# Graph convolution with a highway gate on one core: sort rooms, one visit for the orders, later adding transfers, one flag for two branches

## Chip, cores and metric

The kernel runs on one core of one Trainium2 chip, in one launch. The metric is the device time in microseconds (us) of one execution; for the kernel before, three runs were taken and the median counts. A profiled execution is a further one, with its own time.

## The reference

`x` has N = 1250 rows of D = 1024 floats. There are 20000 edges `src -> dst`, sorted by `dst`, each with one of R = 8 types. Cut to what matters:

```python
h = jnp.maximum(_layernorm(x, axis=-1), 0.0)
u = h @ root + bias
for r in range(R):                        # 8 relations
    mask = (edge_type == r)
    sums = segment_sum(h[src] * mask[:, None], dst, num_segments=N)
    cnt  = segment_sum(mask, dst, num_segments=N)
    u = u + (sums / jnp.maximum(cnt, 1.0)[:, None]) @ weight[r]
z = concatenate([u, h], axis=1) @ w_gate + b_gate
return x + jnp.tanh(u) * z + h * (1.0 - z)
```

## The kernel before

**The products.** Each relation's product `y = h @ weight[r]` is made for all rows first; the edges then gather rows of `y` and add them up with a weight each. There are eleven matrices, numbered `s`: 0 to 7 the relations, 8 `root`, 9 the lower half of `w_gate` (`LAST`), 10 its upper half, which needs `u`. Matrix 0 and matrix 10 go block by block through `product` (five blocks of 256 rows, seven half-size products each, `A11` to `S4`, with the sums `t1` to `t4` of the matrix's quarters as factors). Matrices 1 to 9 go through `kind(m, n, between)`, seven kinds each, written (s, n) here: one kind is one of the seven products of Strassen's scheme for all blocks, and most kinds use the scheme a second time inside. A kind takes about 15.5 us of TensorE time. Its line 330 (`add`) issues the matmuls; line 438 (`tensor_add(banks[2 * u][:, H:], ...)`) adds an inner product onto an accumulator bank on VectorE, which later matmuls of the same kind continue; lines 276 to 283 make the inner sums, line 238 the next factor, lines 346 to 388 move finished banks to rows; line 288 stores and line 296 loads the "lefts", sums of the left operand kept in `lefts_dram`. `store_rows` (line 484) puts finished rows on SyncE's queue.

**What runs beside.** The order of instructions is written out by hand: every `kind` calls `call(k)` for k = 0 to 4, and generators that hang there issue a few instructions at each visit. `at_call` holds the place. In order of time these generators are: the layer norms and the index (`norms_and_index`), the counts of each node's edges per relation (`beside_group`, `counts(g)`), the branch for nodes with more edges than the 22 slots of the table (`counts_over`), the weights of the edges (`weights_of_groups`), and the edges themselves in three groups of relations (`edges(g, ...)`, groups 0, 1, 2), with a gather on GpSimd (line 1407, five buffers `got`) and an add on VectorE (line 1412) for each slot.

**The index.** `order()` sorts the nodes by their number of edges, for each group. Its tiles come from a pool `sort`, opened after the pool `ix0` is closed; so they lie over `raw`, `bits` and `pool_of` of that pool. The table of edges is written from `bits` by one DMA on GpSimd's queue (line 1215). `nodes_in_order` then makes, for one group, an equality matrix on VectorE, waits until `at_call[2] == 2`, turns it with ten matmuls into a bank `ps_q` (line 804), and issues ten gathers of table rows into `idx` (line 728, in `rows_of`). After each group, three or four transfers `out += h` with `accum_op` follow on GpSimd's queue (line 1237, ten in all).

**The flags.** `any_over` reduces, by a transpose on TensorE and a maximum, the largest edge count into `n_far`; `counts_over` loads it into every engine's registers and branches (line 1702) before kind (3,0). Ahead of it, what is left of the counts is issued in one go (lines 1386 and 769 to 774):

```python
            if (s, i) == (BEGIN[0], BEGIN[1] - 1):
                for _ in ready:
                    pass
                counts_over()
```

A second flag `n_pass` is made in `passes_needed` from the weights behind each row's K slots (30 reductions, line 1498) and branches before kind (8,5) (line 1753).

**The gate.** In matrix 9, `beside_kind` loads the quarters of matrix 10 and makes `t1` (line 202), `t2` (line 206), `t3` (line 210) at calls 1, 2, 3 of kind 6; `make_t4` is line 214. In `product`, `p2`, `p3`, `p7` add `A12`, `S4` and `S3`; copies on ScalarE free the bank `ps_b` (lines 612, 628, 636, 639). `gate_h` gathers rows of `h`, `gate_d` makes tanh(u) on ScalarE (line 1857), which writes into a tile that rows of `z` leave by DMA; `gate_turned` transposes `u`, with copies at lines 538 and 540.

Of the kernel before, what the change touches and what calls it, by code (L numbers as in the profile page):

```python
# [21 lines left out]
def tile_rgcn_highway(  # L22
# [139 lines left out]
    class Factors:  # L162
# [12 lines left out]
        def load_first(self, k=slice(0, KQ)):  # L175
# [129 lines left out]
    def kind(m, n, between):  # L305
# [56 lines left out]
        def to_rows_of(odd):  # L362
            of = [(i, banks[i]) for i in (odd, odd + 2)]
            for i, b in of:
# [33 lines left out]
        if chained:  # L398
# [101 lines left out]
    def beside_kind(m, n, k):  # L500
# [15 lines left out]
        elif (n, k) == (5, 0):  # L516
            gate.load_b22()
        elif (n, k) == (6, 0):
            gate.load_b21()
        elif (n, k) == (6, 1):  # L520
            gate.make_t1()
        elif (n, k) == (6, 2):
            gate.make_t2()
        elif (n, k) == (6, 3):
            gate.make_t3()
# [48 lines left out]
    def product(aop, w, to, between=lambda j: None, last=None, pieces=1, second=None, third=None,  # L574
# [76 lines left out]
        else:  # L651
            d = p7()
# [66 lines left out]
    n_pass = const.tile([1, 1], I32, name="n_pass")  # L719
# [59 lines left out]
    def nodes_in_order(g, pos, ids_f, a, b, small, many):  # L779

        a = a[:, :KEYS].rearrange("p (c q) -> p c q", q=P)
        b = b[:, :2 * ND * ND].rearrange("p (c d) -> p c d", d=2 * ND)
        hi_i, lo, hi, block = [small[:, P + k * ND:P + (k + 1) * ND] for k in range(4)]
        hi_i, lo, hi = hi_i.bitcast(I32), lo.bitcast(I16)[:, :ND], hi.bitcast(I16)[:, :ND]
        nc.vector.tensor_copy(block, many[:, :ND])
        nc.vector.tensor_copy(hi_i, pos)  # L788
        nc.vector.tensor_single_scalar(hi_i, hi_i, 7, op=OP.arith_shift_right)
        nc.vector.tensor_copy(hi, hi_i)  # L790
        nc.vector.scalar_tensor_tensor(lo, hi_i, float(-P), pos, op0=OP.mult, op1=OP.add)
        nc.vector.tensor_tensor(a, lo[:, :, None].to_broadcast([P, ND, P]),
                                many[:, None, :].to_broadcast([P, ND, P]), op=OP.is_equal)
        nc.vector.tensor_tensor(b[:, :, :ND], hi[:, :, None].to_broadcast([P, ND, ND]),
                                many[:, None, :ND].to_broadcast([P, ND, ND]), op=OP.is_equal)
        nc.vector.tensor_tensor(b[:, :, ND:], b[:, :, :ND],
                                block[:, :, None].to_broadcast([P, ND, ND]), op=OP.mult)
        nc.vector.tensor_scalar(b[:, :, :ND], b[:, :, :ND], ids_f[:, :1], None, op0=OP.mult)
        yield
        while at_call[2] != 2:  # L800
            yield
        p = sum_bank("ps_q")
        for c in range(ND):
            nc.tensor.matmul(p[:, :2 * ND], a[:, c], b[:, c], start=(c == 0), stop=(c == ND - 1))
        nc.vector.tensor_copy(lo_f := small[:, P + 4 * ND:P + 5 * ND], p[:, :ND])
        nc.vector.scalar_tensor_tensor(node[:, g, :], p[:, ND:2 * ND], float(P), lo_f,
                                       op0=OP.mult, op1=OP.add)
        nc.vector.tensor_single_scalar(node_key[:, g, :], node[:, g, :], g * KEYS, op=OP.add)
        for d in range(ND):
            rows_of(idx[:, g, d, :], table_rows, node_key[:, g, d:d + 1])  # L810
# [113 lines left out]
    def largest(*pairs):  # L924
        p = sum_bank("ps_q")
# [1066 lines left out]
```

## Time and profile before

| | |
|---|---|
| time, median of 3 runs | 1289.37 us (1286.6 to 1289.46) |
| profiled execution, its own time | 1283.34 us |
| span from first to last instruction | 1281.5 us |
| mean granted TensorE clock | 0.996 of full speed |
| TensorE (PE) matmul busy | 1249.9 us, 98% |
| VectorE (DVE) busy | 970.8 us, 76% |
| GpSimd (POOL) busy | 443.7 us, 35% |
| ScalarE (ACT) busy | 274.4 us, 21% |

The profile names engines PE (matmul), PEld (weight load), DVE, ACT, POOL and SP; L438 is line 438 of the kernel before. A row of a timeline gives the start, the busy time, the engine, line and operation, what it writes and reads, how many, and in brackets the idle time just before and what ended it. A row of windows gives the stretch, its length, the busy time of the engines with their instructions, the granted clock (1.00 is full), the mean busy share of the 16 DMA engines and the GB/s moved. A row of waits gives the engine, the waiting instruction's tile and line, what it waited for, and the total in us, the number of times and the longest. The span is 1.8 us shorter than the execution's own time.

### The profile page before, as it was taken

How to read it: one execution, taken by the hardware profiler on the slowest of the kernel's cores; microseconds unless marked ns; L12 is line 12 of the kernel's file. 1: busy time of each engine (PE TensorE's matmuls, PEld its weight loads, DVE VectorE, ACT ScalarE, POOL GpSimd, SP SyncE). 2: the span in 40 equal slices, each digit the busy share in tenths (PEclk: the TensorE clock that was granted, in tenths of full speed). 3: DMA queues.
4: the chain of work that ended last, by engine and by line, in shares of the span. 5: the costliest groups of instructions: out<-in, count | busy, mean ns of one | idle time of the engine just before them, and what ended most of it. 6: DMA issues, size and time to landing. Idle time of an engine off the chain costs nothing.

```text
span 1281.5 us, 14045 instructions
## 1 busy us (share of the span) xinstructions
PE 1249.9 (98%) x4725; PEld 883.1 (69%) x4725; DVE 970.8 (76%) x1462; ACT 274.4 (21%) x517; POOL 443.7 (35%) x400
## 2 busy tenths in 40 slices
PE   9999999899989999999999999999999999999996
PEld 5444777677767777777777777777777777544443
DVE  7545898786579787887878779898888799766642
ACT  3452211121122112112111211211221121202210
POOL 1330000028202222322431333453442558854531
PEclk9999999999999999999999999999999999999999
DMA  7965445838946686898898768899995949999973
GB/s 303 195 191 163 156 149 195 242 107 211 294 149 224 205 280 222 321 335 305 287 341 281 251 197 294 294 331 352 365 301 204 349 141 342 346 333 228 234 150 57
DMA packets 130432, 317.87 MB, mean 248 GB/s; under 512 B 30999, under 2 KB 32222, under 8 KB 130190
## 3 DMA queue, kind: packets, MB, share of 16 engines
q1 hardware_dynamic: 85726, 186.64, 42.7%
q0 software_dynamic: 44336, 129.72, 34.3%
q8 instruction: 38, 0.62, 0.2%
q10 hardware_dynamic: 288, 0.52, 0.1%
q14 instruction: 44, 0.36, 0.1%
HBM read 258.79 MB, written 90.18 MB: 272 GB/s over the span
## 4 chain that ended last, share of the span: by engine, by line
PE 43%; issue 10%; DMA 7%; POOL 7%; DVE 2%; POOLq 0%; ACT 0%; DVEq 0%; SPq 0%; ACTq 0%
PE ps_n L330 14%; PE ps L330 14%; PE ps_b L337 9%; DMA got<-y,idx 5%; PE ps_q L330 4%; POOL got L1407 3%; DMA z_dram<-w 2%; PE ps_b L589 1%; POOL h_all L728 1%; POOL out_dram L739 1%; POOL u L728 1%; PE ps_n L589 1%; POOL w L728 0%; DVE h_all L1412 0%; DVE u L1412 0%
## 5 line engine op out<-in xcount | busy, mean ns | idle before, releaser
L1407 POOL DMA_INDIRECT got<-y,idx x205 | 256.0, 1249 | 435.5 <-DVE u L1412 332.6
L330 PE MATMUL ps<-w,h_all 128*128 128x256 f32 (+1 forms) x1040 | 258.7, 392 | 0.0
L1412 DVE SCALAR_TENSOR_TENSOR u<-got,w_of,u 128x1024 f32<-128x1024 f32 (+1 forms) x189 | 241.5, 1280 | 12.4 <-DMA got<-y,idx 9.8
L330 PE MATMUL ps_n<-w,w 128*128 128x256 f32 x976 | 234.2, 383 | 9.2 <-DVE ps L438 7.3
L330 PEld LDWEIGHTS ps_n<-w,w 128*128 128x128 f32 x976 | 185.0, 191 | 63.2 <-issue 22.2
L337 PE MATMUL ps_b<-w,h_all 128*128 128x512 f32 x504 | 226.6, 592 | 0.0
L330 PEld LDWEIGHTS ps<-w,h_all 128*128 128x128 f32 x1040 | 197.4, 190 | 39.6 <-issue 14.1
L337 PEld LDWEIGHTS ps_b<-w,h_all 128*128 128x128 f32 x504 | 95.8, 190 | 94.1 <-issue 90.9
L589 PE MATMUL ps_b<-w,h_all 128*128 128x512 f32 x312 | 139.4, 593 | 4.4 <-DVE w L206 2.6
L330 PE MATMUL ps_q<-w,w 128*128 128x256 f32 x488 | 116.8, 383 | 5.4 <-DMA w<-lefts_dram 5.4
L448 ACT COPY ps<-ps_n 128x512 f32<-128x512 f32 x122 | 64.8, 575 | 252.5 <-PE ps_n L330 209.1
L330 PE MATMUL ps<-w,w 128*128 128x256 f32 x488 | 115.6, 380 | 0.0
L330 PE MATMUL ps_n<-w,h_all 128*128 128x256 f32 x488 | 115.3, 379 | 0.0
L589 PEld LDWEIGHTS ps_b<-w,h_all 128*128 128x128 f32 x312 | 58.6, 190 | 77.4 <-issue 73.0
L438 DVE TENSOR_TENSOR ps<-ps_n,inner 128x256 f32<-128x256 f32 x122 | 50.5, 430 | 75.0 <-PE ps L330 67.8
L330 PEld LDWEIGHTS ps_q<-w,w 128*128 128x128 f32 x488 | 93.1, 191 | 19.4 <-DVE w L388 4.8
L330 PEld LDWEIGHTS ps<-w,w 128*128 128x128 f32 x488 | 93.1, 191 | 12.8
L330 PEld LDWEIGHTS ps_n<-w,h_all 128*128 128x128 f32 x488 | 92.7, 190 | 13.0 <-issue 0.5
L424 ACT COPY ps<-ps_n 128x256 f32<-128x256 f32 x122 | 39.7, 361 | 247.0 <-PE ps_n L330 178.6
L238 DVE TENSOR_TENSOR w<-w,w 128x2048 f32<-128x2048 f32 x36 | 82.3, 2287 | 0.3
L589 PE MATMUL ps<-w,h_all 128*128 128x512 f32 (+1 forms) x136 | 57.6, 567 | 0.0
L728 POOL DMA_INDIRECT idx<-table,node_key x30 | 32.5, 1082 | 58.6 <-DVE small L788 47.9
(247 smaller groups left out, 1154.8 us busy)
## 6 DMA issues: line engine op xcount, KB each, us to landing
w<-lefts_dram SPq DMA_DIRECT2D x102, 512.0 KB
w<-in_L_gnn_weight_dram SPq DMA_DIRECT2D x31, 1024.0 KB
y<-row SPq DMA_DIRECT2D x84, 256.0 KB
y<-w SPq DMA_DIRECT2D x42, 256.0 KB
w<-in_L_gnn_w_gate_dram SPq DMA_DIRECT2D x8, 1024.0 KB
lefts_dram<-w SPq DMA_DIRECT2D x14, 512.0 KB
h_dram<-h_all SPq DMA_DIRECT2D x9, 512.0 KB
y<-row SPq DMA_DIRECT2D x9, 512.0 KB
```

The source lines that it names most:

```text
L238: nc.vector.tensor_sub(w[to], w[a], w[b])
L330: nc.tensor.matmul(p, a[:, k], b[:, k], start=(fresh and k == 0), stop=(k == a.shape[1] - 1), skip_group_check=True)
L337: nc.tensor.matmul(to, h_op[NP - 1][:, ORDER[n], k], w[:, k], start=(fresh and k == 0), stop=(k == KQ - 1), skip_group_check=True)
L424: nc.scalar.copy(banks[2 * u][:, :H], xs[u])
L438: nc.vector.tensor_add(banks[2 * u][:, H:], xs[u], ys[:, u * H:(u + 1) * H])
L448: nc.scalar.copy(banks[2 * u + 1].rearrange("p (a n) -> p a n", a=2), xs[u][:, None, :].to_broadcast([P, 2, H]))
L589: nc.tensor.matmul(b[:, at], aop[:, i, k, :], w.of[i][:, k, at], start=(fresh and k == 0), stop=(k == KQ - 1), skip_group_check=True)
L728: nc.gpsimd.indirect_dma_start(out=to, out_offset=None, in_=of, in_offset=bass.IndirectOffsetOnAxis(ap=at, axis=0), compute_op=op)
L739: ins = nc.gpsimd.indirect_dma_start(out=of, out_offset=bass.IndirectOffsetOnAxis(ap=at, axis=0), in_=frm, in_offset=None, compute_op=op)
L1407: nc.gpsimd.indirect_dma_start(out=t[:n], out_offset=None, in_=y[g][:, :], in_offset=bass.IndirectOffsetOnAxis(ap=at[:n, d, k:k + 1], axis=0),
L1412: nc.vector.scalar_tensor_tensor(u[:n], t[:n], w, u[:n], op0=OP.mult, op1=OP.add)
```

## The change

The edit has seven parts.

1. The sort's tiles are views of `raw` and of `pool_of` (the latter now allocated next to `bits`), not of a pool of their own; `ix0` is closed after the order.
2. `nodes_in_order` prepares the matrices of all three groups, and turns all of them in one visit, with thirty matmuls into one bank; then the thirty gathers follow, ten a visit.
3. The ten `out += h` transfers are issued by `with_ready`, at each third slot of the edges from slot 12 on, beginning in group 0.
4. `beyond` compares, before the weights are made, the index behind each row's K slots with a constant (fifteen small operations) and takes its maximum into the same `most` column as the edge count; `any_over` sends that column through DRAM to one row (two DMAs on GpSimd's queue), so that `n_far` stands for both branches. The counts are issued one group a visit; `counts_over` is placed before kind (3,1) in place of (3,0); the weights come beside the first slots of group 0.
5. `t1` and `t2` of matrix 10 lie in other buffers, and `t1`, `t2`, `t3` are made at call 3 of kind 5 and calls 1 and 2 of kind 6. A kind without inner scheme empties its second bank one call earlier.
6. `gate_h` and `gate_d` of a block come at j = 5, behind `gate_turned`; block 0's `gate_d` moves into the gate's product.
7. In the last block `p2` comes just before `p7`, not in second place.

```diff
@@ Factors.load_first
-                self.place = dict(b11=old["a"], t3=old["e"], b22=old["b"], t1=old["d"],
-                                  t2=rights, b21=lefts, t4=old["c"])
+                self.place = dict(b11=old["a"], t3=old["e"], b22=old["b"], t1=rights,
+                                  t2=old["d"], b21=lefts, t4=old["c"])
@@ kind, chained part
                 if i == 2:
                     to_rows_of(0)
+                if i == 3:
+                    to_rows_of(1, (0,))
...
-            to_rows_of(1)
+            to_rows_of(1, (2,))
@@ beside_kind
-        elif (n, k) == (6, 1):
+        elif (n, k) == (5, 3):
             gate.make_t1()
-        elif (n, k) == (6, 2):
+        elif (n, k) == (6, 1):
             gate.make_t2()
-        elif (n, k) == (6, 3):
+        elif (n, k) == (6, 2):
             gate.make_t3()
@@ product, last block
         else:
+            p2()
             d = p7()
             last(d, 0)
             p3()
@@ nodes_in_order: all groups prepared, then
+        p = sum_bank("ps_q")[:, :2 * G * ND].rearrange("p (g d) -> p g d", g=G)
+        for g, (a, b, lo_f) in enumerate(parts):
+            for c in range(ND):
+                nc.tensor.matmul(p[:, g], a[:, c], b[:, c], start=(c == 0), stop=(c == ND - 1))
...
+        for g in range(G):
+            for d in range(ND):
+                rows_of(idx[:, g, d, :], table_rows, node_key[:, g, d:d + 1])
+            yield
@@ any_over
-        largest((most[:, 2:3], bad))
+        row = const.tile([1, P], F32, name="bad_row")
+        nc.gpsimd.dma_start(val_dram[0, :P, None], most[:, 2:3])
+        nc.gpsimd.dma_start(row, val_dram[:1, :P])
+        for _ in range(3):
+            yield
+        nc.vector.reduce_max(bad, row, axis=AX.X)
@@ order
-            with tc.tile_pool(name="sort", bufs=1) as sp:
-                counted.extend([sp.tile([P, NHI * NCNT // n], F32, name=f"counted{k}")
...
-                    for d in range(g * ND // G, (g + 1) * ND // G):
-                        nc.gpsimd.dma_start(out[block(d)], h_dram[block(d)], accum_op=OP.add,
-                                            max_dma_last_dim=4 * D)
+            a, b = raw.bitcast(F32), pool_of.bitcast(F32)
+            m = NHI * NCNT
+            counted.extend([a[:, :m], a[:, m:m + m // 2], a[:, m + m // 2:2 * m]])
@@ beside_group
-            yield
             for g in range(G):
-                yield from counts(g)
+                for _ in range(3):
+                    yield
+                for _ in counts(g):
+                    pass
+            yield
+            yield from beyond()
+            yield from any_over()
@@ beyond (new)
+                    nc.vector.tensor_single_scalar(
+                        flags[:, used:used + n].rearrange("p (g d) -> p g d", d=e - d),
+                        idx[:, gs[0]:gs[-1] + 1, d:e, k], float(FAR), op=OP.is_lt)
...
+            nc.vector.reduce_max(most[:, 1:2], flags, axis=AX.X)
+            nc.vector.tensor_max(most[:, 2:3], most[:, 2:3], most[:, 1:2])
@@ the loop over kinds
-            if (s, i) == (BEGIN[0], BEGIN[1] - 1):
-                for _ in ready:
-                    pass
-                counts_over()
-                ready = weights_of_groups()
+        assert next(ready, 0) == 0
+        far = load(n_far)
+        counts_over(far)
+        ready = weights_of_groups()
@@ with_ready
-            for _ in e:
+            for t, _ in enumerate(e):
                 next(ready, None)
+                if added and t > late + GOT and t % 3 == 0:
+                    nc.gpsimd.dma_start(*added.pop(), accum_op=OP.add, max_dma_last_dim=4 * D)
                 yield
@@ second branch
-        passes = nc.values_load(n_pass[0:1, 0:1], ...)
-        with tc.If(passes > 0):
+        with tc.If(far > 0):
@@ gate
-            if i == 0 and j == 4:
-                gate_z(0)
+            if i == 0 and j in (2, 4):
+                (gate_z if j == 4 else gate_d)(0)
...
-            if j == 2:
+            if j == 3:
+                gate_turned(i)
+            elif j == 5:
                 gate_h(i)
-            elif j == 3:
-                gate_turned(i)
                 gate_d(i)
...
-                 (5, 4): lambda: gate_d(0)}
+                 }
```

More of the change, by code (lines that the diff above doesn't have):

```diff
@@ L360, in alone_rows, with to_rows_of @@
                 put(s, i, 1, 0, c21[i])
[L362 to L364 removed]
+        def to_rows_of(odd, only=(0, 2)):
+            for i in [odd + k for k in only]:
+                b = banks[i]
                 if n == 0:
@@ L800, in nodes_in_order @@
         while at_call[2] != 2:
             yield
[L802 to L808, printed above, removed]
@@ L812, in sliding @@
+        for g in range(G):
+            for d in range(ND):
+                rows_of(idx[:, g, d, :], table_rows, node_key[:, g, d:d + 1])
+            yield
     def sliding(t, o, m):
@@ L1337, in index @@
             yield from columns()
+            yield from order()
             first_part.close()
-            yield from order()
-        xh = []
+        xh, added = [], []
         def norms_and_index():
@@ L1346, in norms_and_index @@
                 xh.append((out[block(d)], x[block(d)]))
+                added.append((out[block(d)], h_dram[block(d)]))
             later = index()
@@ L1768, in tile_rgcn_highway @@
                         further(g, d, range(K[g][d], SLOTS), idx[:, g], w_of[:, g])
-            over = nc.values_load(n_over[0:1, 0:1], min_val=0, max_val=E // MORE,
-                                  skip_runtime_bounds_check_because="no more passes than edges")
+            over = load(n_over)
             with tc.If(over > 0):
```

136 lines of the change are left out of this document (59 added, 77 removed).

## The prediction

> **What bounds the kernel now.** I read the page first (span, engines, chain), then PE's waits, then the stretches around its two longest stops, then the rows of the other engines there.
>
> ```profile
> span 1281.5 us, 14045 instructions
> PE 1249.9 (98%) x4725; PEld 883.1 (69%) x4725; DVE 970.8 (76%) x1462; ACT 274.4 (21%) x517; POOL 443.7 (35%) x400
> ```
> ```profile
> PE ps_n L330 <- DVE ps L438: 7.3, 4, 4.7
> PE ps_q L330 <- DMA w<-lefts_dram: 5.4, 3, 4.5
> ...
> PE ps_b L589 <- DVE w L206: 2.6, 1, 2.6
> ...
> PE ps_b L589 <- ACT row L612: 0.9, 1, 0.9
> PE ps_b L589 <- ACT row L639: 0.7, 1, 0.7
> ```
>
> TensorE (PE) is busy for 98% of the span, and the change leaves its products as they are. So an edit is worth only what it takes from PE's 1281.5 − 1249.9 = 31.6 us of idle time, or from time at a lowered clock. The first view gives the ceiling; in the second each row is a wait of PE: total, times, longest. The DMA engines are loaded too, but do not bound it by themselves: a stretch with their share at 1.01 (below) has PE busy for 40.00 of 40 us.
>
> The two longest stops, with the granted clock after them:
>
> ```profile
> 249.11 3.27 PE L330 MATMUL ps_q<-w,w 128*128 128x256 f32 x8 [4.48 <-DMA w<-lefts_dram]
> ...
> 360.26 1.89 PE L330 MATMUL ps_n<-w,h_all 128*128 128x256 f32 x8
> ...
> 375.50 3.43 PE L330 MATMUL ps_n<-w,w 128*128 128x256 f32 x8 [4.74 <-DVE ps L438]
> ```
> ```profile
> 249.00:253.00 4.00, 3.89 (x10) 0.58 0.69 269
> ...
> 375.80:379.30 3.50, 3.50 (x10) 0.51 0.44 136
> ```
>
> Eight matmuls take 1.89 us elsewhere and 3.27 or 3.43 us here. The second windows row has clock 0.51 over 3.5 us, a loss of 3.5 × 0.49 = 1.7 us. So either stop costs about 4.6 + 1.7 = 6.3 us.
>
> **The change, part by part.**
>
> *Sort rooms.* The rank tables move out of a pool laid over the tile `bits`, which a DMA to the table still reads.
>
> ```profile
> 229.38 1.71 POOL L1215 DMA_DIRECT2D table<-bits  x1 [145.97 <-DVE bits L1214]
> ```
> ```profile
> 236.96 0.62 SPq L296 DMA_DIRECT2D w<-lefts_dram  x1
> ```
> ```profile
> 234.33 0.43 DVE L438 TENSOR_TENSOR ps<-ps_n,inner 128x256 f32<-128x256 f32 x1 [0.17 <-PE ps L330]
> 242.12 0.91 DVE L890 TENSOR_TENSOR counted<-runs,counted 128x720 bf16<-128x720 f32 x1 [7.36 <-DMA table<-bits]
> ...
> 247.60 0.69 DVE L283 TENSOR_TENSOR w<-w,w 128x512 f32<-128x512 f32 x1
> ```
>
> DVE's 7.36 us wait goes. But PE's stop is put down to the lefts load, issued at 236.96 while the table transfer was moving and landed just before 249.11; DVE's operand (L283) was ready at 248.29. The load's time hangs on the transfer, which stays. With DVE early, the load is still late: I take 0; the other end is a rival.
>
> *Orders at one visit.* Thirty small matmuls (L804) run in one visit of PE instead of three.
>
> ```profile
> L804 PE MATMUL ps_q<-b,junk x30: 171/171/174, 275.1 to 307.7; 128*128 128x20 bf16 x30
> ...
>   issue: 1.7, 6
> ```
>
> Their count stays. The bounds are 0 and the 1.7 us of switching; most of that lies inside the pipelined busy time, so 0.3. The 30 index gathers come back to back on Pool, ahead of nothing else that PE needs. DVE prepares three groups within one kind instead of one in each of three; what covers that is DVE's free time, 9 us of the 40 in the row of 240–280 below, which the 7.36 us above enlarge. Were it too little, the next L438 would be late by a few us, once; I leave that to the small costs.
>
> *Adding transfers.* Ten transfers out += h, on Pool's queue, move from 293–329 to group 0's edge slots, one each third slot.
>
> ```profile
> L1237 POOL DMA_DIRECT2D out_dram<-h_dram x10: 985/1254/1873, 293.1 to 329.3; - x10
> ```
> ```profile
> 240.00:280.00 40.00, 35.52 (x151) 27.55 (x150) 30.98 (x64) 9.68 (x21) 0.99 (x1) 0.96 0.48 162
> 280.00:320.00 40.00, 39.69 (x185) 31.42 (x184) 26.89 (x55) 6.96 (x15) 32.04 (x31) 1.00 0.79 197
> 320.00:360.00 40.00, 39.62 (x161) 30.00 (x160) 23.94 (x49) 6.22 (x13) 8.44 (x9) 1.00 0.90 275
> 360.00:400.00 40.00, 35.26 (x140) 27.36 (x140) 31.26 (x93) 9.17 (x19) 4.55 (x4) 0.96 0.49 163
> ```
> ```profile
> 400.00:525.00 125.00, 124.77 (x515) 97.51 (x514) 104.72 (x143) 25.49 (x55) 39.88 (x36) 1.00 0.73 240
> ```
> ```profile
> 880.00:920.00 40.00, 40.00 (x166) 31.28 (x165) 34.01 (x49) 6.38 (x14) 17.16 (x18) 1.00 1.01 376
> ```
> ```profile
> PE ps_q L330 <- DMA w<-lefts_dram: 0.4, 1, 0.4
> ```
>
> The last row is PE's only wait between 345 and 348, beside these transfers; it goes: 0.4. Their load, by the excess of the two middle windows over their neighbours (DMA share, second last column): (0.79 + 0.90 − 0.48 − 0.49) × 40 = 29 us of all queues, an upper bound since index gathers are in it. Spread over some 110 us at share 0.73 that makes up to 0.99, which the row at 1.01 carries without a stop. On Pool the ten issues cost 12.5 us, against 85 idle in 125. I take 0.4 for new waits; bounds 0 and 4: DVE's waits for gathers,
>
> ```profile
> DVE h_all L1412 <- DMA got<-y,idx: 24.0, 9, 6.5
> ```
>
> are 24.0 us, and cost PE, late in the span, at most the 2.6 (7.3 − 4.7) of the L438 row; ten transfers of 2.9 us, each waited for in full, would be 29/24 × 2.6 = 3.1, and 4 with PE's waits for ACT.
>
> By the Trainium skill ("DMA: Bandwidth & Descriptors", Queues, rings and completion order) each engine takes turns between queues at packet granularity, so that a transfer on Pool's queue halves a load's rate on SP's and does not stand in front of it. By it the sum is the same; it makes the rival of late loads less likely, though the load issued at 236.96 took 12 us beside the table transfer all the same.
>
> *One flag.* This is the largest term. Now, before kind (3,0)'s L438:
>
> ```profile
> 360.53 0.43 DVE L461 TENSOR_TENSOR ps<-ps,inner 128x256 f32<-128x256 f32 x1 [0.43 <-PE ps L330]
> 361.17 0.91 DVE L1386 MEMSET got<- 128x1024 f32 x1 [0.20 <-issue]
> ...
> 371.50 1.29 DVE L388 TENSOR_TENSOR w<-w,ps 128x512 f32<-128x512 f32 x2 [3.52 <-DVEq L1702]
> ...
> 374.71 0.73 DVE L438 TENSOR_TENSOR ps<-ps_n,inner 128x256 f32<-128x256 f32 x2
> ...
> 376.64 4.61 DVE L238 TENSOR_TENSOR w<-w,w 128x2048 f32<-128x2048 f32 x2
> ```
>
> Two groups' counts (from 361.17 to 371.50 − 3.52 = 367.98, 6.8 us), then the flag's load and branch (3.52), stand ahead of the L438 that PE waits for. After, the counts are spread over kinds (2,4) and (2,5), about 3.4 us a visit, and the If stands one kind later. PE reached (3,0) at 360.26 and came to need L438 at 375.50 − 4.74 = 370.76, 10.5 us in. In (3,1) DVE is free for the branch some 0.7 us after the start, when the second L461 is done (here 360.53 + 0.43). Then follow the branch, 3.5; the reciprocal and two w operations, which with two L388 of 1.2 take the 3.2 from 371.50 to 374.71, so 2.0; the first weights and L438, the 1.9 from 374.71 to 376.64. 0.7 + 3.5 + 2.0 + 1.9 = 8.1 us in, 2.4 before PE's need. So the stop goes entirely: 4.7 + 1.7 = **6.4**. What is late next is the branch's own time; on Pool it took longer:
>
> ```profile
> L1702 POOLq EVENT_SEMAPHORE  x6: 17/30/43, 346.1 to 346.6; - x6
> ...
> L1702 POOLq COMPARE_BRANCH  x1: 53/53/53, 340.9 to 340.9; - x1
> ```
>
> 340.9 to 346.1 is 5.2 us, in the busiest DMA stretch. With 5.2 on DVE the margin is 0.7. The flag itself now goes to DRAM and back in two small DMAs on Pool, ahead of no gather that is due, and DVE reads it in (3,0), in front of that L438. The nearest row is a round trip of the index:
>
> ```profile
> DVE bits L1133 <- DMA bits<-firsts_dram: 4.7, 1, 4.7
> ```
>
> DVE comes to the read some 3.2 us into the kind (0.7, two L388 of 1.2 in all, and at most 1.3 for two w operations), at least three visits after the issue; 10.5 − 3.2 − 0.7 = 6.6 us are left, so even a whole 4.7 us wait there would cost PE nothing. The 30 small reductions (L1498) become fifteen on 1 to 4 columns, beside matmuls: 0. At the second If only the flag's load goes, under 1 us of DVE: 0.
>
> By the Trainium skill ("Runtime: NRT & Kernel Launch", Instruction fetch mechanics) a taken branch to a target outside the fetched window waits for a DMA to fetch it. That speaks against expecting the 3.5 us itself to vanish, and the rows agree: DVE 3.52, Pool 5.2.
>
> *t1, t2, tanh, p2.* All in the last stage.
>
> ```profile
> 1137.96 2.29 DVE L202 TENSOR_TENSOR w<-w,w 128x2048 f32<-128x2048 f32 x1
> 1144.36 1.28 DVE L1412 SCALAR_TENSOR_TENSOR h_all<-got,w_of,h_all 128x1024 f32<-128x1024 f32 x1 [4.12 <-DMA got<-y,idx]
> ...
> 1146.76 2.29 DVE L206 TENSOR_TENSOR w<-w,w 128x2048 f32<-128x2048 f32 x1
> ```
> ```profile
> 1162.30 2.00 ACT L1857 ACTIVATE w<-u 128x1024 f32<-128x1024 f32 x2 [8.81 <-DMA z_dram<-w]
> ```
>
> t2 (L206) stands behind an add that waits 4.12 us for its gather. It takes the place of t1 (L202), which moves to call 3 of that matrix's kind 5: done at 1137.96 + 2.29 = 1140.3 instead of 1149.0, 8.7 us sooner, of which PE waited for 2.6. The 2.6 goes, with 6 to spare. The tanh (L1857), waiting 8.81 us for stores to leave its tile, stands ahead of the copies L540 and L612; behind them, 0.9 goes. The h gathers move with it, from j = 2 to j = 5 of a block's calls: 0. In the last block PE's 0.7 us wait is for a copy (L639) out of the bank that the next product, S3, overwrites; A12's matmuls, eight 512 wide, now go in between: over 3 us, since eight 256 wide take 1.89. The copy is covered and 0.7 goes.
>
> *Sum*: 6.4 + 2.6 + 0.9 + 0.7 + 0.4 + 0.3 = 11.3, less 0.4 = 10.9. The profiled execution is 1281.5 + 1.8 = 1283.3 and would be 1272.4; I subtract the same from the median, 6 us above it: 1289.4 − 10.9 = **1278.5**.
>
> **Rivals.** (a) *The stop at 244.6 goes too*: DVE's earlier work shifts the stores in front, and the lefts load lands in time. For: DVE was ready only 0.8 before PE started, so both are close. Against: the load's issue did not wait for DVE. 10.9 + 6.2 = 17.1, so 1272.3. (b) *The If costs in (3,1) what it cost in (3,0)*: the branch is over 2.4 us longer than 3.52, or the flag comes over 6.6 us late. Pool's 5.2 falls just short. The L438 stop returns and halves the clock again if it is long: gain 10.9 − 6.4 = 4.5, so 1284.9, hardly beyond the 0.3% below. (c) *Slower*: in group 0 an adding transfer holds a lefts load as the table transfer did. Each such event costs 4.5 + 1.7 = 6.2; two of the ten make 1278.5 + 12.4 = 1290.9, three 1297.1. It decides from two events on (they cancel the gain); from three on the kernel is slower by over 0.3%. Against: the same transfers at 293–329 cost one wait of 0.4. (d) *The moves do not reach PE's waits*, because other waits stand just behind in the last stage: half of its 4.2 returns, 1280.6; within the forecast.
>
> **How the numbers follow.** A measurement of this kernel tells about 0.3%, or 3.9 us, from no change. Forecast with (d): 0.62. (a) 0.12; (b) 0.13; (c) 0.07 from two events on; 0.06 for several small costs at once, which would leave 2 to 4 us of gain or less. Faster: 0.62 + 0.12 + 0.08 of (b) = 0.82; same: 0.05 of (b), 0.04 of the small costs, 0.02 of (c) = 0.11; slower: 0.02 of the small costs and 0.05 of (c) = 0.07. The range runs from a little under (a) to a little above (b), and takes in the 4 us bound of the adding transfers: 1270.5 to 1287.
>
> **What would show it.** Right: no L438 wait of PE of over 1 us around 355–380, no clock of 0.5 there, but one after a lefts wait near 244; DVE's row for L890 without its wait; none of the three PE waits of the last stage; DMA share near 0.95 in 400–525 with PE busy throughout. Wrong: a PE wait for lefts between 400 and 525 (c), an L438 wait about 10 us into (3,1) (b), or no lefts wait near 244 (a).

## The result

The changed kernel took 1276.23 us, the median of 5 runs (1273.67 to 1277.68), beside 1287.68 us for the kernel before in the same set of runs (1286.6 to 1289.46). The ratio is 0.9904, 95% interval 0.9888 to 0.992: 11.45 us faster, where 10.9 was forecast. The kernel ran in two more sets. In one the ratio was 0.9924 (0.9899 to 0.9949); in the other the kernel was slower than before, 1.0108 (1.009 to 1.0127), for a reason that the prediction did not have. The experiments come to it.

(In the section on the kernel before, two names are swapped: `gate_h` makes the tanh on ScalarE, and `gate_d` gathers the rows of `h`, which the gather itself adds. So the tanh moves from j = 2, and the gathers of `h` from j = 3.)

The changed kernel's page and PE's waits in it (total, times, longest):

```profile
span 1271.9 us, 14019 instructions
PE 1247.9 (98%) x4723; PEld 881.8 (69%) x4723; DVE 968.5 (76%) x1443; ACT 274.4 (22%) x517; POOL 443.7 (35%) x402
```
```profile
PE ps_q L330 <- DMA w<-lefts_dram: 6.7, 4, 3.9
PE ps_n L330 <- ACT ps L426: 1.9, 6, 0.4
PE ps_n L330 <- DVE ps L440: 1.5, 2, 1.1
PE ps_n L149 <- POOL eps L714: 1.4, 1, 1.4
PE ps_q L535 <- DVE h_all L540: 1.2, 1, 1.2
PE ps L535 <- DVE h_all L1004: 0.8, 1, 0.8
```

Lines have moved: L440 here is L438 of before, L463 is L461, L426 is L424, L540 is L538, L899 is L890, L1223 is L1215, L1409 is L1412, L1740 is L1237. The L438 row fell from 7.3 to 1.5, and the three rows of the last stage (L206 2.6, L612 0.9, L639 0.7) are gone. The lefts row stayed, with the long stop of 3.9 in it, and grew in its small entries: after 900 us they make 2.8 us, where the kernel before has 0.6. The span is 9.6 us shorter than in the execution profiled before (1281.5), and that execution's own time 9.7 (1273.67 against 1283.34).

DVE around the moved branch, and PE there, in the changed kernel:

```profile
365.88 0.27 DVE L946 TENSOR_REDUCE bad<-bad_row 1x1 f32<-1x128 f32 x1 [3.58 <-DMA bad_row<-val_dram]
...
375.00 0.43 DVE L463 TENSOR_TENSOR ps<-ps,inner 128x256 f32<-128x256 f32 x1 [0.43 <-PE ps L330]
381.24 0.20 DVE L1398 TENSOR_SCALAR rcp<-rcp 128x80 f32<-128x80 f32 x1 [5.80 <-DVEq L1702]
...
384.48 0.76 DVE L440 TENSOR_TENSOR ps<-ps_n,inner 128x256 f32<-128x256 f32 x2
```
```profile
374.73 1.89 PE L330 MATMUL ps_n<-w,h_all 128*128 128x256 f32 x8
...
381.64 3.60 PE L337 MATMUL ps_b<-w,h_all 128*128 128x512 f32 x8
385.29 1.99 PE L330 MATMUL ps_n<-w,w 128*128 128x256 f32 x8
```

The branch cost DVE 5.80 us, more than in either row of before (DVE 3.52, Pool 5.2). L440 was done at 384.48 + 0.76 = 385.24, and PE, busy with its L337 matmuls until 385.24, began the next ones at 385.29 without a wait. The stop is gone with nothing to spare.

Its windows (PE busy, clock third from the end, DMA share second from the end):

```profile
360.00:400.00 40.00, 39.94 (x164) 30.75 (x163) 28.55 (x53) 10.21 (x22) 6.37 (x6) 1.00 0.61 181
249.00:253.00 4.00, 4.00 (x12) 3.23 (x11) 0.00 (x0) 0.59 (x1) 0.00 (x0) 0.57 0.64 251
400.00:525.00 125.00, 125.00 (x515) 97.57 (x514) 104.86 (x144) 25.18 (x53) 52.02 (x47) 1.00 0.93 287
304.00:334.00 30.00, 29.64 (x124) 22.94 (x123) 17.51 (x35) 5.14 (x11) 20.37 (x21) 1.00 0.47 133
```

In 360–400 PE has 39.94 of 40 us, against 35.26, at full clock. The half clock near 250 is still there. In 400–525 the adding transfers raise the DMA share from 0.73 to 0.93, and PE is busy for all of the 125 us. The last row, beside the thirty gathers, is for comparison further on.

### The profile page after: what moved, and what is told of

It reads as the page before. It is cut to its first block, busy times and chain, and to the rows that moved or that the text cites. A ratio compares the mean times of both kernels' runs of the same rounds, so it can differ in the third digit from the quotient of the medians.

```text
span 1271.9 us, 14019 instructions
## 1 busy us (share of the span) xinstructions
PE 1247.9 (98%) x4723; PEld 881.8 (69%) x4723; DVE 968.5 (76%) x1443; ACT 274.4 (22%) x517; POOL 443.7 (35%) x402
## 5 line engine op out<-in xcount | busy, mean ns | idle before, releaser
L1409 DVE SCALAR_TENSOR_TENSOR u<-got,w_of,u 128x1024 f32<-128x1024 f32 (+1 forms) x189 | 241.7, 1280 | 22.8 <-DMA got<-y,idx 22.3
L337 PE MATMUL ps_b<-w,h_all 128*128 128x512 f32 x504 | 226.6, 592 | 0.0
L337 PEld LDWEIGHTS ps_b<-w,h_all 128*128 128x128 f32 x504 | 95.8, 190 | 94.1 <-issue 90.9
L440 DVE TENSOR_TENSOR ps<-ps_n,inner 128x256 f32<-128x256 f32 x122 | 50.3, 431 | 77.0 <-PE ps L330 76.9
L426 ACT COPY ps<-ps_n 128x256 f32<-128x256 f32 x122 | 39.8, 360 | 244.7 <-PE ps_n L330 170.6
L730 POOL DMA_INDIRECT idx<-table,node_key x30 | 29.3, 978 | 70.1 <-DVE node L813 61.3
```

What stands on the lines that cost most here:

```text
L337: nc.tensor.matmul(to, h_op[NP - 1][:, ORDER[n], k], w[:, k], start=(fresh and k == 0), stop=(k == KQ - 1), skip_group_check=True)
L426: nc.scalar.copy(banks[2 * u][:, :H], xs[u])
L440: nc.vector.tensor_add(banks[2 * u][:, H:], xs[u], ys[:, u * H:(u + 1) * H])
L730: nc.gpsimd.indirect_dma_start(out=to, out_offset=None, in_=of, in_offset=bass.IndirectOffsetOnAxis(ap=at, axis=0), compute_op=op)
L1409: nc.vector.scalar_tensor_tensor(u[:n], t[:n], w, u[:n], op0=OP.mult, op1=OP.add)
```

## The experiments

There were four sets. Kernels within a set ran on one chip and share the runs of the kernel before; sets 1, 2 and 4 ran on the same chip, set 3 on another.

**The branch alone (set 1).** The kernel before, with only this:

```diff
-            if (s, i) == (BEGIN[0], BEGIN[1] - 1):
-                for _ in ready:
-                    pass
-                counts_over()
-                ready = weights_of_groups()
+        for _ in ready:
+            pass
+        counts_over()
+        ready = weights_of_groups()
```

> The kernel before, with one edit: the first branch stands before kind (3,1) instead of (3,0), so that what is left of the counts is issued one relation a visit during (3,0). Nothing else is changed: transfers, orders, flags and last stage are those of before. Theory: the stop at 370.8 (4.7 us and 1.7 us of slower clock) came from 6.8 us of counts and the branch standing together ahead of the L438; apart, each fits. 1287.7 - 6.4 = 1281.3 us, 0.995. Rival: the branch alone, 3.5 to 5.8 us, with the first weights behind it, makes a stop of its own in (3,1); then the gain is under 3 us and PE waits for L438 there for 1 us or more.

Measured: 1282.64 us against 1288.53, ratio 0.9946 (0.9932 to 0.9961), a gain of 5.9. PE's waits in 255–420, and DVE at the branch:

```profile
PE ps_n L330 <- DVE ps L438: 1.1, 1, 1.1
PE ps_n L330 <- issue: 0.3, 1, 0.3
PE ps_q L330 <- DMA w<-lefts_dram: 0.3, 1, 0.3
```
```profile
387.61 0.20 DVE L1401 TENSOR_SCALAR rcp<-rcp 128x80 f32<-128x80 f32 x1 [4.77 <-DVEq L1702]
```

Over half of the whole gain is this one move, so the theory holds. The rival's wait shows too, but only with 1.1 us: L438 comes a little late in (3,1), with part of the counts still ahead of the branch.

**The counts put back in front of the branch (set 1).** The changed kernel, with the counts of groups 1 and 2 issued in one go ahead of the branch:

```diff
-                for _ in counts(g):
-                    pass
+                if g == 0:
+                    for _ in counts(g):
+                        pass
...
         assert next(ready, 0) == 0
+        for g in range(1, G):
+            for _ in counts(g):
+                pass
```

> The changed kernel, with the counts of groups 1 and 2 issued in one go just ahead of the first branch (which stays before kind (3,1)). Theory: the branch alone leaves L440 a fraction of a microsecond before PE's need (385.2 for about 384.8 in the changed kernel's trace), so that 6.8 us of counts ahead of it come out whole as a stop of PE of some 7 us, and the clock is halved for 3.4 us after it: 1276.2 + 7 + 1.7 = 1284.9 us. Rival: DVE's idle time around the branch takes in a part; the stop is then under 4 us and the time under 1282.

Measured: 1315.21 us, ratio 1.0201 (1.0184 to 1.0218). PE at (3,1), and DVE's branch there:

```profile
423.30 3.78 PE L330 MATMUL ps_n<-w,w 128*128 128x256 f32 x8 [4.66 <-DVE ps L440]
```
```profile
419.25 0.20 DVE L1398 TENSOR_SCALAR rcp<-rcp 128x80 f32<-128x80 f32 x1 [3.66 <-DVEq L1703]
```

The stop came back at the branch, 4.66 us and at half clock behind it (eight matmuls in 3.78), shorter than the 7 expected; the branch itself took 3.66 here against 5.80. So the place of the branch and the spreading of the counts are both needed. The total says nothing on this: of the 26.7 us over the kernel before, the largest part is another stop, of 17.4 us, beside the gathers, which no theory had.

**The table's transfer later (sets 1 and 3).** The changed kernel, with the last operation of the table's rows and the transfer of L1223 five visits later:

```diff
-            nc.vector.scalar_tensor_tensor(rows_in, none, 1.0, rows_in, op0=OP.mult, op1=OP.add)
-            nc.gpsimd.dma_start(table.rearrange("(b p s) o -> p b (s o)", p=P, s=SLOTS), rows_in)
+            edge_rows.append((rows_in, none))
...
-            yield from placing
+            for v, _ in enumerate(placing):
+                if v == TABLE_AT:
+                    ...       # the two statements above
+                yield
```

> The changed kernel, but the last operation that makes the table's rows, and with it the table transfer, comes five visits later, in the middle of kind (2,0), some 21 us after its old place. Theory: PE's stop at 244.5 (3.9 us, and 1.7 us of slower clock) hangs on this transfer, in whose company the lefts load issued at 237.06 took 11.3 us where others take 3.4 to 8.8. Then the load lands in time and the stop goes: 1276.2 - 5.6 = 1270.6 us, clock never at 0.5 between the start and the end. Rival 1: the load is late by its own place, behind a store, two row stores and a weight load on SP's queue; then the stop stays, at 2 to 4 us, and the time is 1276. Rival 2: the transfer holds the next lefts load (issued about 257, needed about 268) as it held this one; the stop moves there and the time is 1276 or more.

Measured: 1298.7 us, ratio 1.007 (1.0054 to 1.0086). PE's waits in 225–300, and the longest one of the whole span:

```profile
PE ps_n L330 <- ACT ps L426: 0.2, 1, 0.2
```
```profile
PE ps L330 <- ACT ps L450: 23.1, 1, 23.1
```

The lefts stop near 248 is gone, so it hangs on the table transfer. But a stop of 23 us stands at 310, as in the kernel above, and hides what that is worth. It was run again in set 3, beside the changed kernel itself:

> The same kernel as table_late, once more: the changed kernel with the table transfer some 21 us later. In its first run PE had no stop at 248, but one of 23 us beside the gathers. Theory A: without that stop, the 4.5 us wait and 1.7 us of slower clock are gone: 6 us under the run beside it, 1271 to 1273 us. Theory B: 1295 to 1301 us again.

Measured: 1297.62 us, ratio 1.0091 (1.0075 to 1.0107), which is the time of theory B: the long stop is there again, with 22.4 us. PE again has no wait for lefts between 225 and 300. The time is 2.9 us less than that of the changed kernel in this set, whose lefts stop was 3.3 us and without a drop of the clock. The two ranges touch (1296.77 to 1298.84, and 1298.69 to 1301.04), so the worth of the later transfer is not measured well.

**The last stage as before (sets 1 and 3).** The changed kernel with the places of `t1` and `t2`, their calls, the emptying of the second bank, `p2`, `gate_h` and `gate_d` put back; some of the lines:

```diff
-        elif (n, k) == (5, 3):
-            gate.make_t1()
         elif (n, k) == (6, 1):
-            gate.make_t2()
+            gate.make_t1()
...
-            p2()
             d = p7()
...
-            elif j == 5:
+            if j == 2:
                 gate_h(i)
```

> The changed kernel with the last stage as before: t1, t2, t3 in their old buffers and at calls 1, 2, 3 of kind 6, the second bank of a kind without inner scheme emptied at its end, tanh and the h gathers at their old places, A12 in second place in the last block. Theory: the three PE waits of the last stage return, 2.6 (t2), 0.9 and 0.7 (copies), 4.2 in all: 1280.4 us. Rival: they stood on gathers that the other edits make come sooner or later, so that about half returns or more than 6 comes; 1278 or 1282 and more.

Measured: 1311.57 us, ratio 1.0173 (1.0155 to 1.0191), again with a 23.1 us stop beside the gathers. Its own part shows in the waits (line numbers as before):

```profile
PE ps L330 <- ACT ps L448: 23.1, 1, 23.1
...
PE ps_b L589 <- DVE w L206: 3.0, 1, 3.0
...
PE ps_b L589 <- ACT row L612: 0.9, 1, 0.9
```

The L639 wait, 0.7, is back too. Run once more beside the changed kernel:

> The same kernel as gate_undone, once more: the changed kernel with the last stage as before. What is open: its 23 us stop beside the gathers, though up to that place its instructions are those of the changed kernel, which had none in two runs. Theory A (the stop belongs to the circumstances of that set of runs, not to the kernel): no stop near 318 now, and the last stage's own price shows: 1280 to 1283 us, 3 to 5 us over the run beside it, with waits of 2.6 (t2), 0.9 and 0.7 (copies). Theory B (it belongs to the program as it is built): 1308 to 1313 us again, 23 us near 318.

Measured: 1305.88 us, ratio 1.0159 (1.0143 to 1.0175), 5.4 us over the changed kernel of that set; 4.2 was forecast for the last stage. Theory A fails for the long stop, which is there again with 20.1 us. The three waits of the last stage are back, but sum to 2.8 us here (1.3, 0.8 and 0.7):

```profile
PE ps_b L589 <- DVE w L206: 1.3, 1, 1.3
```

In the first run they summed to 4.6. By these waits the part is worth 3 to 5 us; the 5.4 is not its price alone.

**The changed kernel again (sets 2 and 3).** Three different edits with the same new stop asked whether the edits or the set made it.

> The changed kernel once more, unedited. Three variants of it had a stop of PE of 17 to 23 us near 310 to 319, where the thirty index gathers run: PE's own signals reached ACT and DVE up to 25 us after the matmuls' ends; the changed kernel's profile has nothing there, nor has the variant of the kernel before. Theory A: the stop is a hazard of thirty gathers back to back, which shows in some executions or on some chips; then this run may show it too, at about 1300 us, and the variants' own edits cost only the rest. Theory B: the edits of the variants bring it; then this run gives 1276 us, 0.990, with no stop over 0.5 us between 250 and 900.

Measured in set 2: 1278.98 us against 1288.77, ratio 0.9924 (0.9899 to 0.9949), and no stop at 310.

> The changed kernel, unedited, beside the next two for comparison: 1276 to 1279 us, no stop over 0.5 us between 255 and 900, a stop of about 4.5 us near 248 behind a lefts load.

Measured in set 3: 1300.52 us (1298.69 to 1301.04) against 1286.11, ratio 1.0108 (1.009 to 1.0127). It is the kernel of the result, without an edit, and its profile has the stop. PE's waits, then PE, ACT with DVE, and Pool at that place, and a window over it. In brackets, `remote` means that a signal ended the wait, but that no end of an instruction lies near that signal:

```profile
PE ps L330 <- ACT ps L450: 23.2, 1, 23.2
PE ps_q L330 <- DMA w<-lefts_dram: 4.8, 3, 3.3
```
```profile
302.43 3.60 PE L337 MATMUL ps_b<-w,h_all 128*128 128x512 f32 x8
307.55 1.99 PE L330 MATMUL ps_n<-w,w 128*128 128x256 f32 x8 [1.53 <-DVE ps L440]
309.38 1.89 PE L330 MATMUL ps<-w,w 128*128 128x256 f32 x8
334.47 2.08 PE L330 MATMUL ps<-w,h_all 128*128 128x256 f32 x4 [23.20 <-ACT ps L450]
```
```profile
319.77 0.59 ACT L351 COPY w<-ps_b 128x512 f32<-128x512 f32 x1 [19.25 <-remote]
333.84 1.06 ACT L450 COPY ps<-ps_n 128x512 f32<-128x512 f32 x2 [13.49 <-remote]
...
333.86 1.28 DVE L378 TENSOR_TENSOR w<-row,ps 128x512 f32<-128x512 f32 x2 [25.05 <-remote]
```
```profile
310.47 0.95 POOL L730 DMA_INDIRECT idx<-table,node_key  x1 [0.30 <-issue]
311.73 0.95 POOL L730 DMA_INDIRECT idx<-table,node_key  x1 [0.30 <-issue]
...
328.05 0.95 POOL L730 DMA_INDIRECT idx<-table,node_key  x1 [0.30 <-issue]
```
```profile
304.00:334.00 30.00, 5.75 (x21) 3.53 (x19) 2.29 (x5) 0.74 (x2) 19.05 (x20) 0.69 0.12 24
```

PE wrote `ps_b` by 302.43 + 3.60 = 306.03. ACT's copy of it (L351) began at 319.77, 13.7 us later. In the result's own profile the same copy comes at once:

```profile
307.04 0.59 ACT L351 COPY w<-ps_b 128x512 f32<-128x512 f32 x1 [6.30 <-PE ps_b L337]
308.81 1.06 ACT L450 COPY ps<-ps_n 128x512 f32<-128x512 f32 x2 [1.19 <-PE ps_n L330]
```

In the window PE has 5.75 of 30 us busy instead of 29.64, DVE 2.29 instead of 17.51, ACT 0.74 instead of 5.14, with the DMA share at 0.12. Only Pool runs on, one gather each 1.25 us; PE begins again at 334.47, some 5 us after the last gather's issue (328.05 + 0.95). So ACT's copy is not held by its data, nor the engines by busy DMA engines. In all six profiles that have the stop, PE begins again 6.0 to 6.4 us after the start of the last gather's issue: the standstill ends when the gathers do.

The trace also holds the times at which semaphores are raised, and they tell what is late. PE's signal for `ps_b` is raised at 319.75, 13.7 us after the matmuls' end, and ACT begins 0.02 us later. The delay grows from signal to signal: five in a row are raised 1.9, 3.2, 4.4, 13.7 and 24.2 us after the ends of their matmuls, and the last three are raised together, at 333.78 to 333.89. DVE's own signals in this stretch are raised 0.01 us after its ends, and in the result's profile PE's are 0.02 us behind theirs. So it is PE's signals that come late, and the other engines stand because they wait for them.

**The adding transfers back among the gathers (set 2).**

```diff
                 rows_of(idx[:, g, d, :], table_rows, node_key[:, g, d:d + 1])
+            for _ in range((3, 3, 4)[g]):
+                nc.gpsimd.dma_start(*added.pop(), accum_op=OP.add, max_dma_last_dim=4 * D)
             yield
```

> The changed kernel, with the ten adding transfers back between the index gathers: three after the first ten, three after the second, four after the third, as before; group 0 has none. Prediction's step: 0.4 us of waits for lefts return and whatever the transfers cost in group 0 goes: 1276 to 1277 us. Theory A (hazard of thirty gathers back to back): the transfers break the row of gathers, so that no long stop shows near 310, whatever the unedited kernel does beside it. Theory B: no difference to the unedited kernel in that place.

Measured: 1283.12 us (1280.61 to 1286.05), ratio 0.9944 (0.9926 to 0.9963), 4.1 us over the unedited kernel of that set (1276.28 to 1281.73), where 1276 to 1277 us was expected. The two intervals of the ratio overlap (the unedited kernel's is 0.9899 to 0.9949). PE's waits in 255–900:

```profile
PE ps_q L330 <- DMA w<-lefts_dram: 2.9, 1, 2.9
PE ps_n L330 <- ACT ps L426: 0.2, 1, 0.2
PE ps_n L330 <- DVE ps L440: 0.2, 1, 0.2
```

PE waited for one lefts load from 366.5 on, where the unedited kernel has no such wait.

**The gathers in three lots of ten (set 2).** Without transfers between them, five visits apart; the counts then follow one visit after another, and what is left of counts and flag is issued just ahead of the branch (these lines are not shown):

```diff
-            nc.vector.tensor_single_scalar(node_key[:, g, :], node[:, g, :], g * KEYS, op=OP.add)
         for g in range(G):
+            nc.vector.tensor_single_scalar(node_key[:, g, :], node[:, g, :], g * KEYS, op=OP.add)
...
-            yield
+            for _ in range(5 if g < G - 1 else 0):
+                yield
```

> The changed kernel, with the gathers issued in three lots of ten, five visits (15.5 us) apart, so that GpSimd pauses some 3 us between lots; the counts follow with fewer visits between, and the flag is read just ahead of the first branch, which may bring a stop of PE of up to 7 us and 1.7 us of slower clock in (3,1). Theory A: no stop near 310 beside the gathers. Theory B: as the unedited kernel. Without a stop in (3,1) 1276 us, with it up to 1285.

Measured: 1305.49 us, ratio 1.0126 (1.0106 to 1.0146), where at most 1285 was expected. No stop at the gathers, but PE itself stood at the branch:

```profile
405.23 1.19 PE L330 MATMUL ps_n<-w,h_all 128*128 128x256 f32 x2 [24.68 <-PEq L1703]
```

The spacing pushed the counts and the flag up to the branch, and PE stands there until the flag is made; DVE alone waits 12.0 us for the flag's row to come back from DRAM. As set 2 has no stop at the gathers for the unedited kernel either, this run does not tell whether lots of ten prevent it. It does show the price of a flag that is late: 24.7 us, all on PE.

**The sort's tiles in a pool again (set 2).**

```diff
-            a, b = raw.bitcast(F32), pool_of.bitcast(F32)
+            with tc.tile_pool(name="sort", bufs=1) as sp:
+                a, b = [sp.tile([P, NHI * WIDE], F32, name=name) for name in ("sort_a", "sort_b")]
...
-            yield from order()
             first_part.close()
+            yield from order()
```

> The changed kernel, with the sort's tiles again in a pool of their own over the closed one, so that DVE waits for the table transfer again (7.4 us near 235). Prediction: DVE's wait returns and PE's stop at 244.5 stays what it is, since the lefts load ends it: no change, 1276 us. Rival: DVE's lateness adds to that stop or to the three groups' preparation in (2,1): a stop longer by 1 to 4 us, or a new wait for L440 in (2,1) or (2,2); 1278 to 1281.

Measured: 1278.27 us, ratio 0.9906 (0.9885 to 0.9926), against 1278.98 for the unedited kernel. DVE's wait is back, and PE's stop near 248 is about the same (5.0, and 4.4 in the unedited kernel), so the prediction's step holds:

```profile
DVE sort_a L899 <- DMA table<-bits: 8.0, 1, 8.0
```
```profile
PE ps_q L330 <- DMA w<-lefts_dram: 5.0, 1, 5.0
```

**The parts together (set 4).** The kernel before with the branch before (3,1), the sort rooms, the last stage as changed, and the table transfer five visits later; the orders stay at three visits with adding transfers between, and the two flags stay separate.

```diff
@@ on the kernel before: the edit of "the branch alone", the last stage of the change, and
-            with tc.tile_pool(name="sort", bufs=1) as sp:
+            av, bv = raw.bitcast(F32), pool_of.bitcast(F32)
...
+            for v, _ in enumerate(placing):
+                if v == TABLE_AT:
```

> The kernel before, with those parts of the change that held in the runs, and without the row of thirty gathers: the first branch before (3,1); sort rooms in the index's own tiles; the last stage as changed (t1, t2, tanh behind copies, A12 before p7); and the table transfer five visits later. Orders at three visits, with the adding transfers between the lots of gathers, and the two flags are those of before. If the 17 to 23 us stop comes only with thirty gathers in a row, this kernel has none, whatever the set of runs. From the kernel before: 5.9 for the branch's place (measured 0.9946), 4.2 for the last stage, 3 to 6 for the table transfer: 13 to 16 us, 1271 to 1274 us, 0.988 to 0.990. Rival: the later transfer or the wider counts bring the waits back elsewhere between 250 and 400; then 1276 to 1282.

Measured: 1271.75 us (1269.34 to 1273.08) against 1288.53, ratio 0.9864 (0.9845 to 0.9883). That is 16.8 us faster than before. The ratio is below the changed kernel's best one (0.9904), though that kernel was not run in this set. PE's longest waits, and the stretch of the gathers:

```profile
PE ps_n L330 <- DVE ps L440: 2.9, 4, 1.1
PE ps L591 <- DVE h_all L573: 2.2, 1, 2.2
PE ps_n L330 <- ACT ps L426: 2.1, 5, 1.0
PE ps_q L330 <- DMA w<-lefts_dram: 1.6, 1, 1.6
```
```profile
304.00:334.00 30.00, 30.00 (x136) 24.03 (x135) 16.87 (x32) 5.14 (x11) 18.98 (x20) 1.00 0.90 233
```

No wait of PE is over 2.2 us, and beside the gathers it is busy for all of the 30 us, at a DMA share of 0.90. But whether set 4 could show the long stop at all is not known: no kernel with thirty gathers in a row ran in it.

## Why the prediction was right, and where not

**The branch and the counts: right, and closer than thought.** The term of 6.4 (4.7 and 1.7 of clock) went, and the branch alone brought 5.9. The steps inside held: L463 done 0.7 us into the kind (375.43 − 374.73), and from the end of the branch to the end of L440 4.0 us (385.24 − 381.24), where 2.0 + 1.9 was worked out. PE came to need L440 10.5 us in, as said (385.24 − 374.73). The term that was off is the branch's own time: 5.80 us instead of 3.5, over the bound of 5.2 from Pool. With 3.66 and 4.77 in the two experiments it differs from profile to profile. Rival (b) needed over 2.4 us more than 3.52; it got 2.3. That the stop went whole, with the branch so much longer than assumed, was luck. The Trainium skill ("Runtime: NRT & Kernel Launch", Instruction fetch mechanics) says that a taken branch waits for a DMA to fetch its target where that lies outside the fetched window. The trace agrees as far as it goes: in each of the four profiles a packet of the instruction queue lies inside DVE's wait (in the changed kernel at 379.17), but whose packet it is, and why the wait moves from 3.5 to 5.8, it does not tell.

**The flag's way through DRAM: right.** DVE waited 3.58 us for it, within the 4.7 taken from the nearest row, and PE lost nothing there.

**The stop near 248: right.** It stayed, at 3.92 us and with the half clock behind it. The sort rooms by themselves are worth nothing that a measurement tells (1278.27 against 1278.98), and the table transfer is what it hangs on, since moving that alone removes it. Rival (a) fell; the stop can go, but by another edit.

**The last stage: right.** Its three waits, 2.6, 0.9 and 0.7, are gone, and undoing the part brought back 4.6 us of them in set 1 and 2.8 in set 3. The wait behind a copy of transposed blocks (L540) grew from 0.5 to 1.2, which gave some of it back, but much less than the half of 4.2 that rival (d) needed.

**The orders' 0.3** is too small to be told in any of the runs.

**The adding transfers: the bounds held, the value is uncertain.** The share in 400–525 rose as worked out (0.93, with 0.99 as the upper bound), PE was busy throughout, and rival (c) fell. By the Trainium skill ("DMA: Bandwidth & Descriptors", Queues, rings and completion order) a transfer on another queue takes turns with a load instead of standing in front; no load in 400–525 was late enough for PE to wait, which agrees. That such a transfer halves a load's rate, as the prediction adds, no run here measures. I netted the move at 0.4 − 0.4 = 0, and putting the ten transfers back cost 4.1. That is about as little as a measurement tells, but the move may be worth more than the 0.4 I gave it. The 0.4 was read where the transfers lay in the kernel before (and at 346, some 17 us after the last of their issues); back among the thirty gathers they went with a wait of PE for a load of 2.9 us. Which transfer held that load is not shown.

**Sum.** From profile to profile, the stops that went are 6.4 (with its clock), 2.6, 0.9, 0.7 and 0.4, together 11.0. The span shows 9.6; the rest is small waits that are new or longer, mostly for lefts late in the span and for the L540 copy. The medians show 11.45. Neither difference is beyond what a measurement tells. That the total came so close is in part luck: the set of the result was one without the stop that follows.

**What failed: "the 30 index gathers come back to back on Pool, ahead of nothing else that PE needs".** In Pool's queue that is true, and yet beside this row the core's other engines can stand still for 17 to 23 us. The prediction gave 0.07 to a slower kernel, but for another reason; it put this cost at nothing. The traces record each time that a semaphore is raised; in the table, "records" is how many such records each trace of a set holds:

| set | records | kernels with thirty gathers in a row | with transfers between lots of ten |
|---|---|---|---|
| profile of before | 13,436 | – | before: none |
| result | 15,262 | changed kernel: no stop | – |
| 1 | 13,566 to 13,612 | table later 23.1, counts put back 17.4, last stage undone 23.1 | before, branch alone: none |
| 2 | 15,254 to 15,263 | changed kernel, sort pool: none | before, transfers put back: none |
| 3 | 13,494 to 13,555 | changed kernel 23.2, table later 22.4, last stage undone 20.1 | before: none |
| 4 | 15,236 | – | before, parts together: none |

The stop's length is that of PE's longest wait in each profile; for "before" the times of each set show it (1286 to 1289 us in all). In set 3 all four runs of the changed kernel lay at 1299 to 1301 us, so within a set it was either there or not. It is no matter of the chip, since sets 1 and 2 ran on the same one, nor of the edits, since the unedited kernel shows both.

The records tell two kinds of set apart, for programs of nearly the same number of instructions (14,013 to 14,054). In the kind with some 13,500 records, all six profiles of a kernel with thirty gathers in a row have the stop; in the other kind none of three has it. So a kernel with transfers between the lots says something only in the first kind. There the kernel before and the branch alone went without a stop (in their profiles one signal of PE beside the gathers is late by some 0.8 us). The kernels with the transfers put back and with the parts together ran only in the second kind, where nothing stopped: they do not show that the transfers protect, nor is it known what they would do in the first. Whether the pauses or the transfers protect, where they do, no run tells either, since the lots without transfers also ran in the second kind. What makes a set one kind or the other, and what holds PE's signals, stays open; that the recording of the traces itself takes part is a rival that no run tests. The prediction's range does not hold for the sets with the stop.

## What to carry to other kernels

When a stop comes from a branch or a serial chain on one engine, add up that engine's time from the start of the kind to the operation that PE needs, for the new place, and ask how much longer the branch may be than its one row shows: here 2.3 of 2.4 us of margin were used. Move an edit's parts one by one on the chip: the place of the branch and the last stage carried most of the gain here, a later table transfer, which takes a stop away, was not in the change, and the single row of gathers came with a risk larger than the whole gain. Before gathers are put into one long row, run the kernel in several sets, because one set may show none of the price; and call a kernel safe only where it ran in a set in which the kernel with the long row does stop.

## What the runs showed that was not expected

- A row of thirty indirect gathers at 1.25 us each can go with a standstill of PE, DVE and ACT of 17 to 23 us (at a DMA share of 0.12 in the changed kernel), in some sets of runs and not in others: the same kernel took 1276, 1279 and 1301 us. PE's signals are what is late, by up to 24 us, and the traces of those sets hold a tenth fewer semaphore records, through most of the span and not only there.
- The same branch cost DVE 3.66, 4.77 and 5.80 us in three profiles, and a late flag held PE at the branch for 24.7 us.
- One table transfer on GpSimd's queue made one load on SyncE's queue late: from its issue at 237.06 to PE's start at 248.47 it is 11.4 us. With the transfer moved, PE waited for no load there:

```profile
237.06 0.50 SPq L296 DMA_DIRECT2D w<-lefts_dram  x1
```
```profile
248.47 3.24 PE L330 MATMUL ps_q<-w,w 128*128 128x256 f32 x8 [3.92 <-DMA w<-lefts_dram]
```
